# Second pass of a graph attention layer: the diagonal blocks transposed by VectorE from squares of 32, and the first block's rows normalized early

## The chip, the cores and the metric

The kernel runs on one core of a Trainium2 chip. The core has a matrix engine (TensorE, PE in the profile, with its weight loads as PEld), a vector engine (VectorE, DVE), an activation engine (ScalarE, ACT), a general engine (GpSimd, POOL), and SyncE (SP), which only issues DMAs here. Each engine works through its own list of instructions in order and waits for others by semaphores. On-chip memory is SBUF, and PSUM for the results of TensorE; DRAM is the large memory outside. Everything is fp32.

The metric is the device time of one run in microseconds, lower is better. Before the change it was 2959.15 us, the median of three runs from 2958.06 to 2962.82.

## The reference, cut to what matters

Two layers run on a matrix x of 4096 rows and 512 columns, with a 4096 x 4096 adjacency matrix. Only layer 0 and the beginning of layer 1 bear on the change:

```
h  = relu(layernorm(x))                      # layer 0
hw = h @ edge_w
e  = hw @ hw.T                               # 4096 x 4096, symmetric
e  = where(adj > 0, e, -9e15)
w  = softmax(h @ node_w, axis=0) * softmax(e, axis=1)
x  = x + (adj * w) @ (h @ weight) + bias
h  = relu(layernorm(x))                      # layer 1 begins
data1 = h @ W.T + b                          # then attention with 8 heads
```

## The kernel before, in words

Rows come in 32 tiles of 128 (P) and 8 blocks of 512 (BL), four tiles to a block (TB).

The first pass (until about 700 us) computes the scores e. As e is symmetric, only the blocks on and above the diagonal are computed and stored in DRAM, as e_d; in a diagonal block, tile row t is stored from its own diagonal tile to the right. The pass also takes the maximum of every row.

The second pass (about 700 to 1600 us) goes over 8 blocks b of 512 output rows, and inside each over the 32 tiles m of the other index: 256 steps. A step needs the scores of tile m against block b with tile m on the partitions. Where m's block lies above (m // TB < b), these are stored as they are needed, and a plain load (L396, tile et) brings them. Where it lies below (m // TB > b), the stored part is the transpose. Then `squares` (L402 to L411) brings four tiles at once with 16 DMAs of 64 KB each into a tile eb, so that every 32 x 32 square already stands at the place where it belongs, and VectorE's transpose, which works inside squares of 32, turns every square (L421, into the PSUM tile pt). In the diagonal block itself, `load` brings the stored upper part of four tiles by L392, also into an eb. The i-th tile of the block needs its first i*128 columns transposed; TensorE does this, one transpose of 128 x 128 for each (L427), 6 in a block.

After that, a step is the same for all: `masks` turns the adjacency tile a (loaded by L399) into 0 or -9e15 (L435); `exps` subtracts the row maximum (L441, in two parts where the tile was half turned), adds the mask (L442) and takes the exponential on ScalarE (L444); `weigh` multiplies by the adjacency (L450, tile at, 3 buffers), and GpSimd adds the exponentials up (L457, L460, tile racc); `gather` does four products of 128 x 128 by 128 x 512 into four PSUM tiles (L480, eight records a step).

The order is written out by hand. At step s each stage is called for a later step, "ahead" of s:

```
stages = ((load, 8), (squares, 9), (turn, 3), (exps, 2), (masks, 3), (weigh, 1), (gather, 0))
```

All engines get their instructions in this order. So at step s VectorE's list has the transpose of s+3, then L441 and L442 of s+2, the mask of s+3, L450 of s+1. All DMAs of loads and squares are on SP's list.

At the end of a block ScalarE copies the four results out of PSUM (L485), and in the next block `finish` scales one tile at a time and adds the residual (L499) and stores it to x1 (L500, on GpSimd's list): at steps 2 to 5 in blocks 1 and 2, at every second step from 2 on in later blocks. For blocks 1 to 6, named by SQ (L511), `finish` also takes the statistics for the layer norm of layer 1 (L505, L506). From step 10 of the following block `layernorm` then computes the square root (L517), scale and shift (L520, L522), the normalized rows (L526) and stores them with four DMAs a tile on SP's list (L532) in DRAM as h_d, again in an order that suits squares of 32.

The tail (about 1600 to 1720 us) is the first linear map of layer 1, one tile t a step: `fetch` (L552) reads h_d where t is in SQ, and x1 elsewhere. Where t is in SQ, `turn_h` is one transpose on VectorE (L577, same operation as L421). Elsewhere, tiles 0 to 3 and 28 to 31, the tail itself does statistics (L558, L560, L562), scale and shift (L568, L570), ReLU (L572), four transposes on TensorE (L583) and a copy from PSUM (L585). `linear` does the product (L591), `values` adds the bias (L598), which releases the PSUM tile; products on GpSimd (L602) and sums on VectorE (L607) follow.

Of the kernel before, what the change touches and what calls it, by code (L numbers as in the profile page):

```python
# [15 lines left out]
P = 128  # L16
# [12 lines left out]
def kernel(  # L29
# [15 lines left out]
    nc = tc.nc  # L45
# [6 lines left out]
    BL = 512  # L52
    NB = N // BL
    TB = BL // P
# [3 lines left out]
    ident = const.tile([P, P], FP, name="ident")  # L58
# [17 lines left out]
    S = 32  # L76
    e_d = dram.tile([N, N + 2 * S], FP, name="e_d")[:, 0:N]
# [23 lines left out]
    with tc.tile_pool(name="w0", bufs=1) as wp, tc.tile_pool(name="a0", bufs=2) as ap_, tc.tile_pool(  # L101
# [32 lines left out]
        def stats(t):  # L134
            st = sp.tile([P, 6], FP, name="st")
            nc.vector.bn_stats(st, xts[t])
            mvs[t] = sp.tile([P, 2], FP, name="mv")
            nc.vector.bn_aggr(mvs[t], st)
            sds[t] = sp.tile([P, 1], FP, name="sd")
            nc.scalar.activation(sds[t], mvs[t][:, 1:2], AF.Sqrt, bias=eps)  # L140

        def norm(t):
            rs = sp.tile([P, 1], FP, name="rs")
            nc.vector.reciprocal(rs, sds.pop(t))
            mr = sp.tile([P, 1], FP, name="mr")
            nc.vector.scalar_tensor_tensor(mr, mvs.pop(t)[:, 0:1], -1.0, rs, op0=ALU.mult, op1=ALU.mult)
            hs[t] = sp.tile([P, F], FP, name="h", bufs=5)
            if t < T0:
                nc.scalar.activation(hs[t], xts[t], AF.Relu, bias=mr, scale=rs)
            else:  # L150
                nc.scalar.activation(squares_of(hs[t]), columns_of(xts[t]), AF.Relu, bias=mr, scale=rs)
# [24 lines left out]
        def turn(t):  # L176
            b, j = divmod(t, TB)
            if j == 0:
                hts[b] = ap_.tile([P, KC, BL], FP, name="h_t")
            if t >= T0:  # L180
                nc.vector.transpose(
                    hts[b][:, :, j * P:(j + 1) * P].rearrange("p k (a q) -> p k a q", q=S),
                    hqs.pop(t).rearrange("p (a k q) -> p k a q", k=KC, q=S))
                return
            h = hs.pop(t)
            pt = pp.tile([P, KC, P], FP, name="pt")
            for k in range(KC):
                nc.tensor.transpose(pt[:, k, :], h[:, k * P:(k + 1) * P], ident)
            nc.vector.tensor_copy(hts[b][:, :, j * P:(j + 1) * P], pt)
            logit(t, h)  # L190
# [25 lines left out]
        def step(t):  # L216
            if t < NT:
                upto(fetch, t + 10 if t >= T0 else t + 7)
                upto(norm, t + 4)
                upto(send, t + 4)  # L220
                turn(t)
                upto(pull, t + 2)
                upto(stats, t + 5)
# [47 lines left out]
    def maxima(i, acc, psum, pool):  # L271

        mx = pool.tile([P, TB], FP, name="mx")
        nc.vector.tensor_reduce(mx, rm[:, i * TB:(i + 1) * TB, i:NB], AX.X, ALU.max)
        pc = psum.tile([P, TB, P], FP, name="pt")
        for j in range(TB):
            nc.tensor.transpose(pc[:, j, :], acc[:, j * P:(j + 1) * P], ident)
        cm = pool.tile([P, TB], FP, name="cm")
        nc.vector.tensor_reduce(cm, pc, AX.X, ALU.max)
        nc.vector.tensor_tensor(mx, mx, cm, ALU.max)  # L280
        yield
        pm = psum.tile([P, BL], FP, name="pt")
        nc.tensor.transpose(pm[:TB, 0:P], mx, ident)
        ms = pool.tile([TB, P], FP, name="ms")
        nc.vector.tensor_copy(ms, pm[:TB, 0:P])
        nc.gpsimd.dma_start(mx_d[i], ms)


    with tc.tile_pool(name="mx", bufs=1) as mxp, tc.tile_pool(name="b_a", bufs=6) as adjp, tc.tile_pool(
# [6 lines left out]
        loaded, masks = {}, {}  # L296
# [52 lines left out]
        for n in range(-6, len(items)):  # L349
# [3 lines left out]
            if n >= 0:  # L353
                i, j, t = items[n]
# [9 lines left out]
    with tc.tile_pool(name="c_a", bufs=11) as adjp, tc.tile_pool(name="c_b", bufs=4) as ebp, tc.tile_pool(  # L364
# [10 lines left out]
        src, pts, aj, mks, ex, at = {}, {}, {}, {}, {}, {}  # L375

        def rows_of(m):
            return slice(m * P, (m + 1) * P)
# [23 lines left out]
        def squares(b, m):  # L402
            cols = slice(b * BL, (b + 1) * BL)
            if m // TB > b and m % TB == 0:
                eb = ebp.tile([P, TB, BL], FP, name="eb")
                sq = e_d[cols, m * P:m * P + BL].rearrange("(a p) (i c q) -> i c p a q", p=S, q=S, i=TB)
                for i in range(TB):
                    for c in range(P // S):
                        nc.sync.dma_start(eb[c * S:(c + 1) * S, i, :].rearrange("p (a q) -> p a q", q=S), sq[i, c])
                for i in range(TB):  # L410
                    src[b, m + i] = eb  # L411

        def turn(b, m):

            i = m % TB
            eb = src[b, m]
            pt = p_t.tile([P, BL], FP, name="pt")
            pts[b, m] = pt
            parts = []
            if m // TB > b:  # L420
                nc.vector.transpose(pt, eb[:, i, :])  # L421
                src[b, m] = [(slice(0, BL), pt)]
                return
            n = i if m // TB == b else 0
            if n > 0:
                for j in range(n):
                    nc.tensor.transpose(pt[:, j * P:(j + 1) * P], eb[:, j, i * P:(i + 1) * P], ident)  # L427
                parts.append((slice(0, n * P), pt))
            if n < TB:
                parts.append((slice(n * P, BL), eb[:, i, :] if m // TB == b else eb))  # L430
            src[b, m] = parts
# [58 lines left out]
        def finish():  # L490

            t, acc, oc, rs, xt = left.pop(0)
            b, j = divmod(t, TB)
            if j == 0:
                sc = sp.tile([P, TB], FP, name="sc")
                nc.vector.reciprocal(sc, rs)
                nc.vector.tensor_tensor(sc, sc, na[:, b * TB:(b + 1) * TB], ALU.mult)
                scale[b] = sc
            nc.vector.scalar_tensor_tensor(oc, acc, scale[b][:, j:j + 1], xt, op0=ALU.mult, op1=ALU.add)  # L499
            nc.gpsimd.dma_start(x1[rows_of(t), :], oc)  # L500
            if t in SQ:
                if j == 0:
                    mv4[b] = sp.tile([P, TB, 2], FP, name="mv4", bufs=1), []
                st = sp.tile([P, 6], FP, name="st", bufs=4)
                nc.vector.bn_stats(st, oc)  # L505
                nc.vector.bn_aggr(mv4[b][0][:, j, :], st)  # L506
                mv4[b][1].append(oc)

        SQ = range(TB, (NB - 1) * TB)  # L511
        mv4 = {}

        def layernorm(b):
# [35 lines left out]
        def fetch(t):  # L550
            xl[t] = etp.tile([P, BL], FP, name="et")
            nc.sync.dma_start(xl[t], h_d[t] if t in SQ else x1[rows_of(t), :])  # L552

        def stats(t):
            if t in SQ:
                return
# [7 lines left out]
        def norm(t):  # L564
            if t in SQ:
                return
# [7 lines left out]
        def turn_h(t):  # L574
            if t in SQ:
                hts[t] = wkp.tile([P, BL], FP, name="d")
                nc.vector.transpose(hts[t].rearrange("p (k a q) -> p k a q", k=KC, q=S),  # L577
                                    xl.pop(t).rearrange("p (a k q) -> p k a q", k=KC, q=S))
                return
            h = hs.pop(t)  # L580
            pt = p_t.tile([P, BL], FP, name="pt")
            for k in range(KC):
                nc.tensor.transpose(pt[:, k * P:(k + 1) * P], h[:, k * P:(k + 1) * P], ident)  # L583
            hts[t] = wkp.tile([P, BL], FP, name="d")
            nc.scalar.copy(hts[t], pt)  # L585
# [27 lines left out]
        end = len(steps)  # L613
# [35 lines left out]

        stages = ((load, 8), (squares, 9), (turn, 3), (exps, 2), (masks, 3), (weigh, 1), (gather, 0))
        for s in range(-9, end):
            for f, ahead in stages:
                if 0 <= s + ahead < end:
                    f(*steps[s + ahead])
                if f is weigh:
                    b, m = divmod(s, NT)
                    if left and m > 1 and (m % 2 == 0 or b < 3):
                        finish()  # L660
                    if m == 10 and b - 1 in mv4:
                        norms = layernorm(b - 1)
                    if m >= 10:
                        next(norms, None)
                    tail(s - end)
                    if s == 3:
                        ending = maxima(NB - 1, acc_z, p_t, sp)
                    if s in (3, 4):
                        next(ending, None)
# [10 lines left out]
        pt = p_t.tile([P, BL], FP, name="pt")  # L680
# [50 lines left out]
    with tc.tile_pool(name="p", bufs=2) as prp, tc.tile_pool(name="rl", bufs=2) as rlp, tc.tile_pool(  # L731
# [321 lines left out]
        stages = ((load, 3), (logs, 5), (exps, 1), (weigh, 1), (factors, 2), (scale, 2), (gather, 0))  # L1053
# [47 lines left out]
```

## Time and profile before

One execution was profiled. Its page and its trace are the source of all times here.

| | |
|---|---|
| median of three runs | 2959.15 us |
| the profiled execution | 2957.07 us |
| its span | 2955.3 us |
| PE busy | 2911.4 us, 99% |
| DVE busy | 2534.6 us, 86% |
| POOL busy | 1380.0 us, 47% |
| ACT busy | 1325.5 us, 45% |
| L480 PE, x2048 | 887.2 us |
| L427 PE, x48 | 9.1 us, 274 ns each |
| L421 DVE, x112 | 80.6 us, 719 ns each |
| L577 DVE, x24 | 16.8 us, 699 ns each |
| L409 SP, squares, x448 | 64 KB each |
| granted TensorE clock | 0.995 |

Busy time is the sum over an engine's instructions. A matmul's recorded length is longer than its share of TensorE's time, because matmuls overlap: L480's 2048 records have a mean of 594 ns, yet fill 887.2 us. What a stage costs is therefore read from the distance between starts, and from the idle times, which the timeline shows in brackets with what ended them. A clock below 1 means that TensorE was granted only that share of its full rate.

### The profile page before, as it was taken

How to read it: one execution, taken by the hardware profiler on the slowest of the kernel's cores; microseconds unless marked ns; L12 is line 12 of the kernel's file. 1: busy time of each engine (PE TensorE's matmuls, PEld its weight loads, DVE VectorE, ACT ScalarE, POOL GpSimd, SP SyncE). 2: the span in 40 equal slices, each digit the busy share in tenths (PEclk: the TensorE clock that was granted, in tenths of full speed). 3: DMA queues.
4: the chain of work that ended last, by engine and by line, in shares of the span. 5: the costliest groups of instructions: out<-in, count | busy, mean ns of one | idle time of the engine just before them, and what ended most of it. 6: DMA issues, size and time to landing. Idle time of an engine off the chain costs nothing.

```text
span 2955.3 us, 42955 instructions
## 1 busy us (share of the span) xinstructions
PE 2911.4 (99%) x15179; PEld 1137.7 (38%) x15179; DVE 2534.6 (86%) x3584; ACT 1325.5 (45%) x1822; POOL 1380.0 (47%) x1043
## 2 busy tenths in 40 slices
PE   8999999999999999999999989999999999999998
PEld 4444444444444444444444423323222322232222
DVE  5435777778888998998996789999999999999998
ACT  2211111111121221221221068888777777777776
POOL 3401111113444444444444756565757575757574
PEclk9999999999999999999999999999999999999999
DMA  5525666667876766756653259696969696979795
GB/s 181 172 78 200 223 218 225 226 218 187 205 178 162 177 161 187 186 166 180 190 167 127 61 152 242 187 258 188 256 191 249 194 250 204 243 202 243 208 232 153
DMA packets 485160, 570.89 MB, mean 193 GB/s; under 512 B 265080, under 2 KB 315288, under 8 KB 484944
## 3 DMA queue, kind: packets, MB, share of 16 engines
q1 hardware_dynamic: 431920, 406.70, 45.8%
q0 software_dynamic: 51008, 157.51, 23.2%
q10 hardware_dynamic: 2016, 3.93, 0.4%
q8 instruction: 119, 1.95, 0.3%
q14 instruction: 97, 0.79, 0.1%
HBM read 415.76 MB, written 72.55 MB: 165 GB/s over the span
## 4 chain that ended last, share of the span: by engine, by line
PE 92%; DVE 4%; ACT 2%; DMA 1%; issue 1%; SPq 0%; POOL 0%; DVEq 0%; ACTq 0%; POOLq 0%
PE po L480 29%; PE pv L881 27%; PE pe L331 15%; PE dn L886 9%; PE po L591 4%; PE ps L196 3%; PE pe L203 3%; DVE pr L849 2%; PE pt L936 1%; ACT e L817 1%; DMA acc<-pr 1%; DMA xt<-in_x_dram 0%; DVE acc_z L154 0%; DVE pt L441 0%; PE pt L920 0%
## 5 line engine op out<-in xcount | busy, mean ns | idle before, releaser
L881 PE MATMUL pv<-pr,sup 128*32 128x512 f32 x8192 | 1010.0, 594 | 9.0 <-POOL d_m L1046 5.4
L480 PE MATMUL po<-sup,at 128*128 128x512 f32 x2048 | 887.2, 594 | 3.8 <-DVE at L450 3.8
L858 POOL TENSOR_TENSOR acc<-acc,pr 128x1024 f32<-128x1024 f32 x232 | 558.2, 2406 | 318.1 <-DVE pr L849 317.8
L849 DVE SCALAR_TENSOR_TENSOR pr<-z,g_m,ex 128x1024 f32<-128x1024 f32 x512 | 631.0, 1273 | 5.2 <-ACT ex L807 4.1
L480 PEld LDWEIGHTS po<-sup,at 128*128 128x128 f32 x2048 | 387.1, 190 | 483.2 <-issue 446.3
L460 POOL TENSOR_TENSOR racc<-racc,ex 128x512 f32<-128x512 f32 x240 | 362.3, 1510 | 385.3 <-ACT ex L444 383.8
L881 PEld LDWEIGHTS pv<-pr,sup 128*32 128x32 f32 x8192 | 286.7, 110 | 593.2 <-issue 533.6
L444 ACT ACTIVATE ex<-d 128x512 f32<-128x512 f32 x256 | 160.5, 630 | 624.7 <-DVE d L442 616.5
L331 PE MATMUL pe<-he_t,he_t 128*128 128x512 f32 x896 | 386.4, 592 | 0.0
L807 ACT ACTIVATE ex<-e 128x1024 f32<-128x1024 f32 x256 | 263.0, 1027 | 227.2 <-DVE pr L849 226.6
L849 DVE SCALAR_TENSOR_TENSOR pr<-z,g_m,e 128x1024 f32<-128x1024 f32 x256 | 328.9, 1285 | 9.9 <-PE pv L881 5.9
L886 PE MATMUL dn<-pr,d_m 128*2 128x512 f32 x1984 | 335.6, 592 | 0.0
L817 ACT ACTIVATE e<-e,ld_m 128x1024 f32<-128x1024 f32 x256 | 291.0, 1137 | 6.5 <-DMA e<-in_adj_t_dram 6.3
L846 DVE SCALAR_TENSOR_TENSOR pr<-rl,ngd_m,ex 128x1024 f32<-128x1024 f32 x224 | 285.0, 1273 | 1.6 <-ACT ex L807 1.2
L835 ACT ACTIVATE rl<-z,ngd_m,d_m 128x1024 f32<-128x1024 f32 x224 | 275.0, 1228 | 0.0
L450 DVE TENSOR_TENSOR at<-ex,a 128x512 f32<-128x512 f32 x256 | 189.5, 740 | 71.1 <-ACT ex L444 48.0
L331 PEld LDWEIGHTS pe<-he_t,he_t 128*128 128x128 f32 x896 | 169.2, 190 | 210.1 <-issue 190.5
L335 POOL DMA_DIRECT2D e_d<-es x144 | 78.4, 545 | 364.8 <-ACT es L334 359.2
L334 ACT COPY es<-pe 128x512 f32<-128x512 f32 (+2 forms) x144 | 79.1, 550 | 377.2 <-PE pe L331 377.2
L442 DVE TENSOR_TENSOR d<-pt,mk 128x512 f32<-128x512 f32 x256 | 177.0, 691 | 8.8
L336 DVE CUSTOM_DVE_ANT_0 mk<-pe,mk 128x512 f32<-128x512 f32 (+2 forms) x144 | 93.0, 645 | 98.9 <-ACT es L334 98.8
L435 DVE TENSOR_SCALAR mk<-a 128x512 f32<-128x512 f32 x256 | 128.5, 502 | 2.2 <-DMA a<-in_adj_t_dram 2.2
(186 smaller groups left out, 2564.9 us busy)
## 6 DMA issues: line engine op xcount, KB each, us to landing
e<-in_adj_t_dram SPq DMA_DIRECT2D x256, 512.0 KB, 5.5
acc<-pr POOLq DMA_DIRECT2D x152, 512.0 KB, 5.7
a<-in_adj_t_dram SPq DMA_DIRECT2D x256, 256.0 KB, 3.8
ar<-in_adj_dram SPq DMA_DIRECT2D x120, 256.0 KB, 3.0
e_d<-es POOLq DMA_DIRECT2D x120, 256.0 KB, 3.1
eb<-e_d SPq DMA_DIRECT2D x456, 64.0 KB, 3.0
ac<-in_adj_t_dram SPq DMA_DIRECT2D x112, 256.0 KB, 3.5
et<-e_d SPq DMA_DIRECT2D x112, 256.0 KB, 3.8
```

The source lines that it names most:

```text
L331: nc.tensor.matmul(pe[:, :w], he_t[i][:, k, (t % TB) * P:(t % TB + 1) * P], he_t[j][:, k, BL - w:], start=(k == 0), stop=(k == KC - 1))
L450: nc.vector.tensor_tensor(w, e, aj.pop((b, m)), ALU.mult)
L460: nc.gpsimd.tensor_tensor(racc, racc, e, ALU.add)
L480: nc.tensor.matmul(po[j], w[:, j * P:(j + 1) * P], sup[:, m, :], start=(m == 0), stop=last)
L807: nc.scalar.activation(x_, ra.pop((i, m)), AF.Exp)
L817: nc.scalar.activation(x_, ra[i, m], AF.Exp, bias=ld_m[:, h // HG, m:m + 1])
L835: nc.scalar.activation(r, zs_[i, 0], AF.Relu, bias=ngd_m[:, h // HG, m:m + 1], scale=d_m[:, h, m:m + 1])
L846: nc.vector.scalar_tensor_tensor(w, rl.pop((i, m)), ngd_m[:, h // HG, m:m + 1], x_, op0=ALU.subtract, op1=ALU.mult)
L849: nc.vector.scalar_tensor_tensor(w, zs_[i, k], g_m[:, h + k, m:m + 1], e3.pop((i, m)) if k == 3 else x_, op0=ALU.max, op1=ALU.mult)
L858: nc.gpsimd.tensor_tensor(acc[i, 3], acc[i, 3], w, ALU.add)
L881: nc.tensor.matmul(v[c][q][r * D + c0:r * D + c0 + Q, :], va[:, m, g * HG + k, c0:c0 + Q], pr[i, m, k][:, q * BL:(q + 1) * BL], start=(m = ...
L886: nc.tensor.matmul(dn[r * Q:r * Q + w.shape[1], :], w, src[:, q * BL:(q + 1) * BL], **fl)
```

## The change

Three things change, all in the second pass and the tail.

First, the diagonal blocks get what the blocks below it had. For tile i of a diagonal block (i = 1, 2, 3), `squares` now issues four DMAs of i*16 KB on SP, which bring the stored part above the diagonal as squares of 32 into the unused left part of the same eb. `turn` calls VectorE's transpose on the first i*128 columns, in place of i transposes on TensorE.

Second, `squares` is called 8 steps ahead in place of 9, so that it follows `load` of the same step, which makes the tile eb that it fills; the loop starts at -8.

Third, SQ now begins with tile 0. The rows of block 0 get their statistics in `finish` and are normalized and stored to h_d in block 1; the tail reads h_d for tiles 0 to 3 and turns them on VectorE. Tiles 28 to 31 stay as they were.

```diff
@@ squares
+            if m // TB == b and m % TB > 0:
+                i = m % TB
+                sq = e_d[b * BL:b * BL + i * P, m * P:(m + 1) * P].rearrange("(a p) (c q) -> c p a q", p=S, q=S)
+                for c in range(P // S):
+                    nc.sync.dma_start(
+                        src[b, m][c * S:(c + 1) * S, i, 0:i * P].rearrange("p (a q) -> p a q", q=S), sq[c])
@@ turn
-            if m // TB > b:
-                nc.vector.transpose(pt, eb[:, i, :])
-                src[b, m] = [(slice(0, BL), pt)]
-                return
-            n = i if m // TB == b else 0
+            n = TB if m // TB > b else i if m // TB == b else 0
             if n > 0:
-                for j in range(n):
-                    nc.tensor.transpose(pt[:, j * P:(j + 1) * P], eb[:, j, i * P:(i + 1) * P], ident)
+                nc.vector.transpose(pt[:, 0:n * P], eb[:, i, 0:n * P])
                 parts.append((slice(0, n * P), pt))
@@
-        SQ = range(TB, (NB - 1) * TB)
+        SQ = range((NB - 1) * TB)
@@
-        stages = ((load, 8), (squares, 9), (turn, 3), (exps, 2), (masks, 3), (weigh, 1), (gather, 0))
-        for s in range(-9, end):
+        stages = ((load, 8), (squares, 8), (turn, 3), (exps, 2), (masks, 3), (weigh, 1), (gather, 0))
+        for s in range(-8, end):
```

## The prediction

> **What bounds the kernel now.** I read four views, in this order: the chain of work that ended last, the TensorE timeline of the stretch that the change touches (from 697 us to 1722 us), the VectorE timeline around the places where TensorE stops, and SP's timeline at the start of the second pass. The chain of the whole page:
>
> ```profile
> PE 92%; DVE 4%; ACT 2%; DMA 1%; issue 1%; SPq 0%; POOL 0%; DVEq 0%; ACTq 0%; POOLq 0%
> ```
>
> The TensorE timeline says where TensorE is not the bound. Columns are start, length, engine, line, operation, then the idle time before it and what ended that:
>
> ```profile
> 705.75 12.85 PE L480 MATMUL po<-sup,at 128*128 128x512 f32 x24 [2.25 <-DVE at L450]
> ...
> 826.42 3.60 PE L480 MATMUL po<-sup,at 128*128 128x512 f32 x8
> 829.86 0.38 PE L427 MATMUL pt<-ident,eb 128*128 128x128 f32 x2
> 830.07 3.60 PE L480 MATMUL po<-sup,at 128*128 128x512 f32 x8
> 833.51 0.49 PE L427 MATMUL pt<-ident,eb 128*128 128x128 f32 x3
> 833.84 92.87 PE L480 MATMUL po<-sup,at 128*128 128x512 f32 x216
> ...
> 952.14 3.70 PE L480 MATMUL po<-sup,at 128*128 128x512 f32 x8 [0.40 <-DVE at L450]
> ...
> 957.17 3.70 PE L480 MATMUL po<-sup,at 128*128 128x512 f32 x8 [1.10 <-DVE at L450]
> ...
> 1604.45 5.40 PE L591 MATMUL po<-eb,d 128*128 128x512 f32 x8 [1.85 <-ACT d L585]
> ```
>
> TensorE runs without a gap except at four places: before the first product of the pass, twice in block 2, where VectorE's L450 is late, and at the hand-over to the tail. A step of eight products takes 3.43 us (92.7 us for 27 steps in the chain). From 826.42 to 830.07 is 3.65 and from 830.07 to 833.84 is 3.77, so one L427 transpose costs TensorE 0.11 us and not its recorded 0.27.
>
> The third view is VectorE's timeline in blocks 1 and 2:
>
> ```profile
> 826.96 1.86 DVE L441 TENSOR_TENSOR pt<-eb,mb 128x384 f32<-128x384 f32 x1
> ...
> 834.78 0.71 DVE L421 STREAM_TRANSPOSE pt<-eb 128x512 f32<-128x512 f32 x1
> 835.40 0.53 DVE L441 TENSOR_TENSOR pt<-pt,mb 128x384 f32<-128x384 f32 x1
> ...
> 937.70 0.69 DVE L505 BATCH_NORM_STATS2 st<-oc 128x6 f32<-128x512 f32 x1
> 938.43 0.18 DVE L506 BATCH_NORM_AGGREGATE mv<-st 128x2 f32<-128x6 f32 x1
> ```
>
> A 384-wide L441 with both inputs in SBUF takes 1.86 us where 0.57 is its undisturbed time (703.47). POOL's L460 runs from 827.11 to 828.39 in its timeline, and L441 ends 0.4 us after it. Whatever VectorE does just before such a collision is free until POOL is done.
>
> **What the Trainium skill says.** "SBUF — State Buffer", section "SBUF: two separate sides": VectorE and GpSimd share a port pair as an exclusive lock, and a VectorE operation with two SBUF inputs blocks for the whole of a GpSimd operation that reads SBUF. The 1.86 us agrees. "TensorE: Matmul & The Clock Gate", Part 1: a free-running activity window of 3.413 us decides the clock, which halves after an idle window. The trace agrees: the clock is 0.50 from 705.75 to 710.40 and 0.69 from 1605 to 1610. Part 4 of that page: transposes do not count as busy for this. The hand-over fits, for it went to half clock although eight transposes ran inside its gap. "VectorE: DVE Perf Modes", "The three transpose paths": VectorE transposes only within 32x32 blocks, so the block order has to come from elsewhere. Here that is the squares DMA.
>
> **The change part by part.** Everything below is against the profiled run: 2957.07 us, its span 2955.3.
>
> *TensorE's diagonal transposes go.* There are 6 per block (1+2+3), 0.11 us each: 0.66 us a block, 5.3 us in all where TensorE is the bound. In block 0 all six ran before 705.75, while TensorE was waiting, so nothing comes back there.
>
> *VectorE's transposes come.* The 128x512 row is 720 ns, 0.63 us start to start. No narrower one is in the trace. By a straight quarter the first would be 0.18 us; if the fixed part of L441's widths (295, 428, 544, 668 ns) holds, 0.32. I take 0.23, 0.37 and 0.50 start to start, 1.1 us a block.
>
> *Twelve more DMAs a block on SP* (four each of 16, 32 and 48 KB). Issues there take 0.43 us (L532) to 0.53 us (spacing of the 64 KB squares when nothing holds them): 5 to 6.4 us a block.
>
> *Statistics of block 0 in block 1.* L505 and L506 lengthen a finish from 0.66 to 1.6 us, four times, 3.8 us. On ScalarE there are two table loads of 1.28 us and four L526 of 0.8, on VectorE two small operations of 0.4 us, on SP 16 stores of 0.43 us. In block 2 the same work (ScalarE 969 to 993) brings no gap on TensorE after 961. I cost it at nothing beyond the 3.8 us.
>
> *Squares at 8 ahead.* Each 16-DMA group goes one step (3.43 us) later. In block 1 the group of m=24 would now follow a store that waits for L526, and starts near 871 us. Its first four land near 877 (2.1 issue, 3.0 landing), and VectorE needs them near 889: 12 us of cover.
>
> Now by place.
>
> Block 0. VectorE reaches L450 for the first product at 705.01, now behind two more transposes: 0.6 us later. The half clock ends when a busy window ends, on average half a window plus one later, 5.1 us instead of 4.65: 0.2 us more. SP issues in this stretch without rest:
>
> ```profile
> 695.00 13.07 SPq L409 DMA_DIRECT2D eb<-e_d  x16
> 708.12 1.91 SPq L399 DMA_DIRECT2D a<-in_adj_t_dram  x4
> ```
>
> With twelve issues and a4 ahead, the group of m=4 ends near 714, so mask tile a5 is issued there and lands near 717.5 (3.4 to 3.8 us). VectorE wants it at 715.4, then delivers product 3 at 718.6; TensorE needs it at about 718.9. This just fits. I put block 0 at +0.9, from +0.5 to +4.
>
> Block 1. Here L450 has little lead: for product 7 it ends at 842.5, the product starts at 844.13. I walked VectorE through the steps with the added work. The second transpose and the first statistics end at 827.5, inside POOL's lock until 828.39: free. The third adds nothing before 833.3 for the same reason. From then on each finish costs its 0.95 more: L450 for product 6 ends at 840.0 (needed 840.04, TensorE now being 0.66 earlier), for product 7 at 844.6 (needed 843.47). That is a stall of 1.2 us; later steps have VectorE at 2.87 against 3.43. Net +0.5. If nothing were hidden it would be +3; with no stall, -0.7.
>
> Block 2. L450 for product 7 stays at 956.43, as the transposes fall into L441's waits (1.84, 1.37, 1.12). Only the last 0.33 us is gained: -0.3.
>
> Blocks 3 to 7. In block 3 L450 is 0.4 to 2 us ahead at the diagonal, and each extra transpose is covered by that or by a lock. 5 x 0.66 = -3.3.
>
> Hand-over. The last product ends at 1601.76, the last L499 at 1602.5. Now come reciprocal, statistics, L572 on ScalarE, eight transposes, L585 and at 1604.45 L591. After: L577 on VectorE right behind L499 (699 ns), L591 at about 1603.25: -1.2. The transposes of the next two tiles, 8 x 0.11: -0.9. The gap without products was 2.7 us and becomes 1.5. Block 2's waits of 0.40 and 1.10 us, 1.6 us with the transposes, did not lower the clock, so I take it that this one does not either. The first eight L591 then take 3.6 instead of 5.4: -1.8. Together -3.9; -2.1 if the clock drops all the same. VectorE's L577 for the third tile follows L598 and ends two microseconds ahead of its product.
>
> Sum: 0.9 + 0.5 - 0.3 - 3.3 - 3.9 = -6.1 us, so 2951.0 for a run like the profiled one. The median shown is 2.1 us above that run; the same -6.1 gives 2953.0.
>
> **The rivals.**
> The clock falls at the hand-over after all. For it: a window that holds the whole gap is busy for 56% only (1.9 of 3.413 us). Counting windows from 710.40, where full clock returned, the one from 956.2 to 959.6 held 2.4 us of products (71%) and the clock stayed; the one from 1601.3 to 1604.7 held 0.7 (20%) and it fell. It gives 2954.8.
> SP is late in block 0. For it: single issues of 2.09 us there while the DMA engines are over 90% busy. Against it: a4 now goes out before the big group instead of behind it. Every microsecond that a5 is later than 717.8 is a microsecond of stall; at 2 to 5 us it gives 2955 to 2958.
> More is hidden. Block 1's stall does not arise (+0.5 becomes -0.7) and block 0 starts no later: 2950.9.
> Slower: the squares become late. SP's load with stores, in blocks 1 and 2, is 16 x 0.53 + 4 x 0.47 + 8 x 0.43 = 13.8 us per four steps of 13.7 us, so lost lead is not won back while the stores last. If groups issue at block 0's 0.82 us, they take 18.4, and over two groups nearly the 12 us of cover are gone. From there every microsecond stops VectorE's L421, then TensorE. It ends slower when about 12 us of stall come together in the blocks with both; 2966. Against it: the trace shows 0.82 only in the first group, and 8.4 to 9.6 us for a group in block 1.
>
> **How the numbers follow.** Chances: as worked out 0.45, clock falls 0.20, SP late 0.17, more hidden 0.10, squares late 0.08. Under 0.2% (5.9 us) is about what a measurement of this kernel can't tell from no change. The likeliest case lies on that line: a little over half of it is faster (0.25), with 0.02 of the second and all 0.10 of the fourth: 0.37. Slower: 0.08 and 0.01 of SP's tail. Same: 0.54. The likeliest case alone spans 2951 to 2955; the range takes in the fourth below and SP's late start above, 2950 to 2960.5.
>
> **What would show it.** No L427; 48 L421 at widths of 128, 256 and 384, 0.2 to 0.6 us. TensorE's line unbroken around the diagonal of blocks 3 to 7, those blocks 0.66 us shorter. A stall by L450 of about 1 us in block 1 near product 7. L591 starting 1.5 us after the last L480, at full clock. Wrong would be: waits of L421 or L435 on DMAs past 720 us, a first L480 more than 1 us later, or stalls in blocks 3 to 7.

## The result, and the profile after

The changed kernel takes 2953.49 us, the median of 18 runs (2950.86 to 2954.88); on the same chip the kernel before takes 2957.82 us, the median of 18 runs (2954.96 to 2962.82). The ratio is 0.9984, with an interval from 0.9978 to 0.9991: some 4.3 us faster, between 2.7 and 6.5. The predicted time was 2953.0. The gain of 0.16% is below the 0.2% that the prediction called hard to tell from no change; with 18 runs of each, the interval excludes 1. The profiled execution took 2953.74 us, with a span of 2951.9 us.

The first view is again the chain of work that ended last:

```profile
PE 80%; DVE 8%; issue 5%; DMA 3%; ACT 2%; POOL 1%; SPq 0%; DVEq 0%; POOLq 0%; ACTq 0%
```

TensorE's share fell from 92% to 80%. That is not the change: 4 points each were lost in L331 of the first pass (15% to 11%) and in L881 of the later attention (27% to 23%, now L882), where the code is the same and the chain went through other engines this time. TensorE is busy for 98% of the span, against 99%. The chain can't show a change of this size, so I read TensorE's timeline of the second pass (columns: start, length, engine, line, operation, then the idle time before it and what ended it). From L435 on all line numbers are one higher than before; L416 are the new DMAs, and L428 is VectorE's transpose (L421 before). "Product 7" stands for the products of step 7 of a block, eight records, so x256 are 32 steps.

```profile
705.45 13.21 PE L481 MATMUL po<-sup,at 128*128 128x512 f32 x24 [6.12 <-DMA eb<-e_d]
...
815.18 0.95 PE L478 MATMUL rs<-ones,racc 128*128 128x1 f32 x8
815.99 27.85 PE L481 MATMUL po<-sup,at 128*128 128x512 f32 x64
845.05 82.67 PE L481 MATMUL po<-sup,at 128*128 128x512 f32 x192 [1.22 <-DVE at L451]
...
953.16 3.70 PE L481 MATMUL po<-sup,at 128*128 128x512 f32 x8 [0.51 <-DVE at L451]
...
958.18 82.67 PE L481 MATMUL po<-sup,at 128*128 128x512 f32 x192 [1.32 <-DVE at L451]
...
1090.28 62.07 PE L481 MATMUL po<-sup,at 128*128 128x512 f32 x144 [0.47 <-DVE at L451]
...
1152.99 110.11 PE L481 MATMUL po<-sup,at 128*128 128x512 f32 x256
...
1601.24 38.03 PE L592 MATMUL po<-eb,d 128*128 128x512 f32 x88 [1.46 <-DVE d L578]
```

No transpose is left among the products. Block 4 is one unbroken run of 256 records (1152.99); before, the diagonal's transposes cut every such run. Two waits are new: one in block 1, before product 7, and one in block 3, before product 13. The bracket of the first product of the pass names a DMA, but the product starts 0.06 us after L451 on VectorE ends (704.71 to 705.39).

The two traces are compared piece by piece, by landmarks on TensorE that both kernels have: the last L283 of the first pass, the row sums at the end of each block (before L477, after L478), and the first transpose L645 (after L646) behind the first linear map's beginning.

| piece, us | before | after | measured | predicted |
|---|---|---|---|---|
| block 0 | 115.23 | 116.12 | +0.89 | +0.9 |
| block 1 | 111.42 | 112.38 | +0.96 | +0.5 |
| block 2 | 113.46 | 113.13 | -0.33 | -0.3 |
| block 3 | 111.42 | 111.50 | +0.08 | -0.66 |
| blocks 4 to 7 | 445.80 | 443.10 | -2.70 | -2.64 |
| hand-over | 47.66 | 43.82 | -3.84 | -3.9 |
| sum | 945.00 | 940.05 | -4.95 | -6.1 |

What lies outside these pieces holds the same code, and moves by itself: the first pass ended 0.84 us earlier, and from that L646 to TensorE's last instruction it took 2.4 us longer (1303.40 against 1300.97; the other runs below lie between 1301.08 and 1303.8). A single pair of spans therefore says nothing at the level of one microsecond. The pieces do.

What makes the new wait in block 1 stands in VectorE's timeline:

```profile
821.46 0.32 DVE L428 STREAM_TRANSPOSE pt<-eb 128x128 f32<-128x128 f32 x1
821.69 1.53 DVE L442 TENSOR_TENSOR pt<-eb,mb 128x512 f32<-128x512 f32 x1
...
827.25 0.46 DVE L428 STREAM_TRANSPOSE pt<-eb 128x256 f32<-128x256 f32 x1
827.62 0.27 DVE L442 TENSOR_TENSOR pt<-pt,mb 128x128 f32<-128x128 f32 x1
827.92 0.97 DVE L442 TENSOR_TENSOR pt<-eb,mb 128x384 f32<-128x384 f32 x1
...
839.40 0.68 DVE L451 TENSOR_TENSOR at<-ex,a 128x512 f32<-128x512 f32 x1
...
841.51 0.18 DVE L507 BATCH_NORM_AGGREGATE mv<-st 128x2 f32<-128x6 f32 x1
842.04 0.73 DVE L428 STREAM_TRANSPOSE pt<-eb 128x512 f32<-128x512 f32 x1 [0.35 <-DMA eb<-e_d]
...
844.31 0.68 DVE L451 TENSOR_TENSOR at<-ex,a 128x512 f32<-128x512 f32 x1
```

GpSimd's timeline has, at the second transpose:

```profile
827.17 1.28 POOL L461 TENSOR_TENSOR racc<-racc,ex 128x512 f32<-128x512 f32 x1
```

The transposes of 128 and 256 columns take 0.32 and 0.46 us, and the next instruction starts 0.23 and 0.37 us after they do. Those start-to-start costs are the ones that the prediction took. The second one is free, as predicted: L442 behind it now takes 0.97 us where it took 1.86, and ends 0.44 us after GpSimd's L461 (827.17 to 828.45), as before (0.43). So the port lock of "SBUF — State Buffer", "SBUF: two separate sides", pays for it. L451 for product 7 ends at 844.99, and the product starts at 845.05. One wait was not foreseen: VectorE stood still for 0.35 us before 842.04. The bracket puts it down to a DMA of squares, but the four DMAs that this transpose reads were issued by 813.8 and had landed by 815.8. They belong to the first of these groups on SP's list:

```profile
808.50 9.51 SPq L409 DMA_DIRECT2D eb<-e_d  x16
818.11 1.86 SPq L399 DMA_DIRECT2D a<-in_adj_t_dram  x4
820.02 9.56 SPq L409 DMA_DIRECT2D eb<-e_d  x16
```

What landed at 842 was a later group. The cause of this stop is open.

The bracket of 1.22 us counts from the recorded end of the product before, which overhangs. From product 31 of block 0 (815.99) to product 7 are 29.07 us, and 27.55 in a kernel below whose block 1 has no wait. So product 7 is 1.52 us late, and product 8 loses 0.10 more, as after the waits in blocks 2 and 3: 1.62 us in all.

### The profile page after: what moved, and what is told of

The parts are those of the page before. It is cut to its first block, busy times and chain, and to the rows that moved or that the text cites. A ratio compares the mean times of both kernels' runs of the same rounds, so it can differ in the third digit from the quotient of the medians.

```text
span 2951.9 us, 43009 instructions
## 1 busy us (share of the span) xinstructions
PE 2904.7 (98%) x15115; PEld 1135.7 (38%) x15115; DVE 2541.1 (86%) x3606; ACT 1324.7 (45%) x1817; POOL 1376.2 (47%) x1043
## 4 chain that ended last, share of the span: by engine, by line
PE 80%; DVE 8%; issue 5%; DMA 3%; ACT 2%; POOL 1%; SPq 0%; DVEq 0%; POOLq 0%; ACTq 0%
PE po L481 27%; PE pv L882 23%; PE pe L331 11%; PE dn L887 8%; DVE pr L850 4%; PE po L592 4%; PE ps L196 3%; PE pe L203 3%; DMA acc<-pr 2%; DVE pt L442 1%; POOL e_d L335 1%; PE pt L937 1%; DVE pr L847 1%; POOL acc L859 1%; ACT e L818 0%
## 5 line engine op out<-in xcount | busy, mean ns | idle before, releaser
L882 PE MATMUL pv<-pr,sup 128*32 128x512 f32 x8192 | 1008.9, 594 | 10.1 <-POOL d_m L1047 5.6
L481 PE MATMUL po<-sup,at 128*128 128x512 f32 x2048 | 885.4, 594 | 9.6 <-DMA eb<-e_d 6.1
L481 PEld LDWEIGHTS po<-sup,at 128*128 128x128 f32 x2048 | 388.5, 190 | 498.4 <-issue 452.8
L461 POOL TENSOR_TENSOR racc<-racc,ex 128x512 f32<-128x512 f32 x240 | 357.4, 1489 | 385.4 <-ACT ex L445 384.0
L882 PEld LDWEIGHTS pv<-pr,sup 128*32 128x32 f32 x8192 | 289.0, 110 | 592.8 <-issue 526.3
L331 PE MATMUL pe<-he_t,he_t 128*128 128x512 f32 x896 | 386.4, 592 | 0.0
L331 PEld LDWEIGHTS pe<-he_t,he_t 128*128 128x128 f32 x896 | 169.2, 190 | 210.1 <-issue 190.5
L451 DVE TENSOR_TENSOR at<-ex,a 128x512 f32<-128x512 f32 x256 | 187.5, 732 | 71.0 <-ACT ex L445 45.9
L442 DVE TENSOR_TENSOR pt<-et,mb 128x512 f32<-128x512 f32 x112 | 127.5, 1138 | 0.0
```

The source lines that it names most:

```text
L331: nc.tensor.matmul(pe[:, :w], he_t[i][:, k, (t % TB) * P:(t % TB + 1) * P], he_t[j][:, k, BL - w:], start=(k == 0), stop=(k == KC - 1))
L451: nc.vector.tensor_tensor(w, e, aj.pop((b, m)), ALU.mult)
L461: nc.gpsimd.tensor_tensor(racc, racc, e, ALU.add)
L481: nc.tensor.matmul(po[j], w[:, j * P:(j + 1) * P], sup[:, m, :], start=(m == 0), stop=last)
L882: nc.tensor.matmul(v[c][q][r * D + c0:r * D + c0 + Q, :], va[:, m, g * HG + k, c0:c0 + Q], pr[i, m, k][:, q * BL:(q + 1) * BL], start=(m = ...
```

## The experiments

Two theories stood at first. Theory A is the prediction's: the change in the diagonal gives 0.11 us per transpose wherever TensorE is the bound, and the stall of block 1 comes from the statistics of block 0's rows. Theory B holds VectorE's new transposes responsible for the stall.

### One part alone: the diagonal

In the changed kernel, block 0's rows are left to the tail again:

```diff
-        SQ = range((NB - 1) * TB)
+        SQ = range(TB, (NB - 1) * TB)
```

> The changed kernel without the rows of block 0 (SQ from tile 4 again). From block start to block start (L478 to L478) the changed kernel takes 112.38 us for block 1, the kernel before 111.42. Theory A, the stall of block 1 comes from the statistics of block 0, while the diagonal transposes hide behind GpSimd's lock: no wait for L451 in block 1, the block 110.8 us. Rival B, the stall comes from the transposes' VectorE time: a wait of 1 us or more stays, the block about 112. Both: block 0 0.9 us longer than before, blocks 4 to 7 at 110.75, the hand-over (last L478 to L646) 47.7 as before. In all about 2.5 us faster than before under A, 1.5 under B.

2953.92 us, the median of 21 runs, against 2958.03 (41 runs) of the kernel before; ratio 0.9987, from 0.9981 to 0.9994. TensorE's timeline has no listed wait in block 1:

```profile
816.15 110.37 PE L481 MATMUL po<-sup,at 128*128 128x512 f32 x256
...
1601.26 3.70 PE L592 MATMUL po<-eb,d 128*128 128x512 f32 x8 [1.85 <-ACT d L586]
```

Block 1 took 111.01 us: 0.41 less than before and 1.37 less than with both parts. It is not quite down to the 110.76 of an undisturbed block. The missing 0.25 us are again at product 7: its L451 ends at 843.79, the product starts 0.15 us late, too little to be listed, and product 8 loses the 0.10. So the listed stall needs the statistics, and Theory B falls as the whole cause. With the transposes alone 0.25 us of stall are left.

The second line is a surprise. With the old form of the hand-over and the same gap of 1.85 us as before, the first eight products took 3.70 us, not 5.40. The clock did not fall, and the hand-over took 45.96 us in place of 47.66. More on this below.

### One part alone: the rows

In the kernel before, SQ begins with tile 0; the diagonal stays on TensorE and the squares stay 9 steps ahead.

```diff
-        SQ = range(TB, (NB - 1) * TB)
+        SQ = range((NB - 1) * TB)
```

> The kernel before with the rows of block 0 alone (SQ from tile 0, TensorE's transposes kept, squares 9 ahead). Theory A: block 1 has a wait of 0.5 to 0.8 us for L450 at product 7, the block about 112.1 us in place of 111.42. Rival B: no wait, 111.4. Both: block 0 as before (115.2 from the last L283 to the first L477), blocks 4 to 7 as before at 111.45, the hand-over at 43.8 in place of 47.7, its first products at full clock. In all about 3 us faster than before.

2955.14 us (13 runs) against 2958.03; ratio 0.999, from 0.9982 to 0.9998. Block 1 keeps its transposes on TensorE, and waits less, because TensorE itself is later:

```profile
843.94 82.67 PE L480 MATMUL po<-sup,at 128*128 128x512 f32 x192 [0.32 <-DVE at L450]
```

Block 1 took 112.01, blocks 4 to 7 from 111.42 to 111.57 as before, and the hand-over 43.82, exactly that of the whole change. So the hand-over's gain belongs to the rows and the gain of blocks 4 to 7 to the diagonal. By the medians the two parts are faster by 4.1 and 2.9 us alone and by 4.3 together. That they are worth less together than their sum is mainly block 1: the stall at product 7 is 0.25 us with the transposes alone, 0.59 with the statistics alone and 1.62 with both.

### The remaining gap at the hand-over

In the changed kernel the first two tiles of the tail are turned ahead of the last `finish` calls, and not in the tail's first step:

```diff
+        turn_h(0)
+        turn_h(1)
         while left:
             finish()
...
-                if s == 0:
-                    turn_h(0)
-                if s + 1 < NT:
+                if 0 < s and s + 1 < NT:
```

> The changed kernel with the first two transposes of the tail (L578) moved on VectorE's list ahead of the four L500 of the last block; VectorE is idle for 6.9 us there. If the gap of 1.46 us ahead of the first L592 is the wait for VectorE's list, it goes, since the first L592 then waits only for the first L500: the hand-over 42.4 us in place of 43.8, the kernel 1.5 us faster than the changed one. Rival: L592 also waits for the later L500s through the PSUM tiles or for the load of w1, and the gap stays above 1 us.

2950.27 us (9 runs) against 2958.03; ratio 0.9974, from 0.9964 to 0.9984. VectorE's timeline, and then TensorE's:

```profile
1589.14 1.30 DVE L578 STREAM_TRANSPOSE d<-et 128x512 f32<-128x512 f32 x2
```

```profile
1595.93 3.68 PE L481 MATMUL po<-sup,at 128*128 128x512 f32 x8
1599.45 25.91 PE L592 MATMUL po<-eb,d 128*128 128x512 f32 x60
```

L592 follows the last L481 without a gap, and the hand-over takes 42.09 us, 1.73 less. In the changed kernel both transposes stand behind the four L500, although their rows had been in DRAM since block 1:

```profile
1597.24 3.33 DVE L500 SCALAR_TENSOR_TENSOR oc<-po,sc,xt 128x512 f32<-128x512 f32 x4 [0.59 <-PE po L481]
1600.48 1.29 DVE L578 STREAM_TRANSPOSE d<-et 128x512 f32<-128x512 f32 x2
```

The gap of 1.46 us is thus made by the order of VectorE's list alone.

### Finishes two steps apart

In blocks 1 and 2 `finish` ran at every step from 2 to 5; here it runs at every second step, as in the later blocks:

```diff
-                    if left and m > 1 and (m % 2 == 0 or b < 3):
+                    if left and m > 1 and m % 2 == 0:
```

> The changed kernel with finish at every second step from step 2 on in blocks 1 and 2 too, as in the later blocks. Theory A: VectorE is late in blocks 1 and 2 because four finishes with statistics come in four steps; spread out, the waits for L451 in both blocks go: block 1 110.8 us in place of 112.38, block 2 111.3 in place of 113.13, the kernel 3.4 us faster than the changed one. Rival: at steps 6 and 8 of block 1 the steps have full transposes and VectorE has only 0.56 us to spare in each, so the wait only moves: block 1 stays above 111.5.

2949.32 us (9 runs) against 2958.03; ratio 0.9976, from 0.9967 to 0.9986.

```profile
816.19 110.11 PE L481 MATMUL po<-sup,at 128*128 128x512 f32 x256
...
965.56 72.37 PE L481 MATMUL po<-sup,at 128*128 128x512 f32 x168 [0.59 <-DVE at L451]
```

Block 1 is one run of 256 records, 110.76 us, 1.62 less than in the changed kernel; block 2 takes 111.62, 1.51 less, with one wait left. The stalls of both blocks come from four finishes in a row, each with its statistics on VectorE. With 0.95 us more at every second step the work fits in the lead.

### A wider gap and the clock

The prediction had put 1.8 us of the hand-over down to the clock: a gap of 2.7 us lets it fall, one of 1.5 us does not. In the changed kernel VectorE turns the tail's first tile twice more, with the same result, before the second:

```diff
                 if s == 0:
                     turn_h(0)
+                    for _ in range(2):
+                        nc.vector.transpose(hts[0].rearrange("p (k a q) -> p k a q", k=KC, q=S),
+                                            x_0.rearrange("p (a k q) -> p k a q", k=KC, q=S))
```

> The changed kernel with the first transpose of the tail done three times over on VectorE (same result), which makes the gap ahead of the first L592 about 2.75 us in place of 1.46, near the 2.7 us without products of the kernel before. Theory A: the half clock after the gap belongs to the gap's length; the first eight L592 take 5.4 us and the hand-over 46.9 us (43.8 + 1.3 + 1.8). Rival B: it is decided by where the gap falls against free-running windows, so that with the same length it can come or not; without it the hand-over is 45.1 us. One run can show B and not exclude it.

One run, 2953.36 us, against 2957.01 (9 runs). TensorE's timeline, and then its window from 1605 to 1610 (stretch, length, then busy time and instructions of PE, PEld, DVE, ACT and POOL, the granted clock, the DMA share, GB/s), of this kernel:

```profile
1603.23 22.16 PE L592 MATMUL po<-eb,d 128*128 128x512 f32 x51 [2.96 <-DVE d L639]
```

```profile
1605.00:1610.00 5.00, 5.00 (x13) 2.28 (x12) 1.31 (x2) 0.00 (x0) 2.25 (x2) 1.00 0.33 106
```

The same window of the kernel before:

```profile
1605.00:1610.00 5.00, 5.00 (x11) 2.14 (x10) 0.12 (x1) 0.00 (x0) 0.00 (x0) 0.69 0.16 54
```

With 2.96 us without products the clock stayed at 1.00; in the trace of before, with 2.7 us from the recorded end of the last L480 to the first L591, it fell to half until 1608. The hand-over took 45.32 us, which is the 43.82 plus the 1.50 of the longer gap. So the length of the gap alone doesn't decide the fall, and 1.8 us are not saved in every run.

### Block 0 left on TensorE

In block 0 the diagonal is turned by TensorE, without the 12 DMAs of squares; all else is the change.

```diff
-            if m // TB == b and m % TB > 0:
+            if m // TB == b > 0 and m % TB > 0:
...
-                nc.vector.transpose(pt[:, 0:n * P], eb[:, i, 0:n * P])
+                if m // TB == b == 0:
+                    for j in range(n):
+                        nc.tensor.transpose(pt[:, j * P:(j + 1) * P], eb[:, j, i * P:(i + 1) * P], ident)
+                else:
+                    nc.vector.transpose(pt[:, 0:n * P], eb[:, i, 0:n * P])
```

> The changed kernel with the diagonal transposes of block 0 alone on TensorE again and without their 12 DMAs. Theory: two transposes ahead of the first L451 on VectorE's list cost block 0 0.53 us, and the rest of its 0.9 is the half clock. The first product then starts 5.86 us after the last L283 in place of 6.39, and the piece from L283 to the first L478 is 115.2 to 115.6 us in place of 116.1. Rival: SP's 12 more DMAs make it late; then the first product is no earlier, but waits on mask tiles after 712 us in the changed kernel would be gone.

One run, 2949.87 us, against 2957.01 (9 runs). Its lines from L435 on stand four further down than in the changed kernel.

```profile
705.02 12.13 PE L485 MATMUL po<-sup,at 128*128 128x512 f32 x24 [2.25 <-DVE at L455]
...
843.19 82.67 PE L485 MATMUL po<-sup,at 128*128 128x512 f32 x192 [0.87 <-DVE at L455]
```

The first product comes 5.86 us after L283, as in the kernel before, and not 6.39. Block 0 takes 114.51 us, less than was expected, since the half clock here lasted 3.41 us and 6.83 in all other profiles. The bracket in block 1 falls from 1.22 to 0.87 us, by the 0.35 us that VectorE stood still before 842.04; that stop is gone. It stands before the same transpose in both other kernels whose block 1 is that of the change (841.92 with the early turns, 842.47 with the wider gap). In this kernel VectorE's list is another one from block 0 on. It fits that the stop goes with the list; why it comes is not shown.

### Squares 8 steps ahead, alone

In the kernel before only the distance is changed:

```diff
-        stages = ((load, 8), (squares, 9), (turn, 3), (exps, 2), (masks, 3), (weigh, 1), (gather, 0))
-        for s in range(-9, end):
+        stages = ((load, 8), (squares, 8), (turn, 3), (exps, 2), (masks, 3), (weigh, 1), (gather, 0))
+        for s in range(-8, end):
```

> The kernel before with the squares 8 steps ahead in place of 9 and nothing else. By the prediction it costs nothing, since the first transfers of a group land 12 us before they are needed: all blocks within 0.1 us of the kernel before (115.2 or 115.5 for block 0, then 111.4, 113.5, 111.4, 111.4), no wait of L421 on a DMA. Rival: VectorE's L421 waits on squares in blocks 1 or 2, which are then more than 0.3 us longer.

One run, 2959.5 us, against 2957.01 (9 runs from 2955.79 to 2961.46). Blocks 1 to 7 take what they took before, within 0.03 us, and VectorE waits for no DMA between 700 and 930 us. What makes the total higher lies outside the pass: its first pass ended at 701.57 and the rest took 1303.8 us. So the shorter distance costs nothing by itself. This is also the third hand-over in the old form, and the clock stayed again:

```profile
1605.78 3.70 PE L591 MATMUL po<-eb,d 128*128 128x512 f32 x8 [1.86 <-ACT d L585]
```

It took 45.97 us, as in the kernel with the diagonal alone.

### All waits at once

Finishes two steps apart, the tail's first turns ahead of the last finishes, block 0 on TensorE, and the layer norm of the rows from step 20 of a block instead of 10 (lines again four further down):

```diff
-                    if m == 10 and b - 1 in mv4:
+                    if m == 20 and b - 1 in mv4:
...
-                    if m >= 10:
+                    if m >= 20:
```

> The changed kernel with the four repairs together: finish at every second step, the layer norm's scale and rows from step 20 of a block on in place of 10, the tail's first two transposes ahead of the last four L500, block 0's diagonal on TensorE. If the waits seen in the changed kernel are all there is between it and an unbroken TensorE, block 1 is 110.8, block 2 110.8 to 111.1, block 3 110.8, the hand-over 42.1, block 0 115.2 to 115.6: 6.9 us less than the changed kernel, a ratio to the kernel before of about 0.996. Rival: moved statistics and rows meet the later steps with full transposes and waits for L451 show up there.

2947.69 us (5 runs, 2945.54 to 2948.41) against 2957.01 (9 runs); ratio 0.9965, from 0.9951 to 0.9978. It is the fastest kernel measured here.

```profile
814.27 110.11 PE L485 MATMUL po<-sup,at 128*128 128x512 f32 x256
...
963.69 72.37 PE L485 MATMUL po<-sup,at 128*128 128x512 f32 x168 [0.64 <-DVE at L455]
...
1036.70 110.11 PE L485 MATMUL po<-sup,at 128*128 128x512 f32 x256
...
1594.02 37.93 PE L596 MATMUL po<-eb,d 128*128 128x512 f32 x88
```

The pass takes 933.7 us, 6.35 less than with the change and 11.3 less than before (1.7 of these are the clock of the hand-over, which fell in one profile of three). One wait is left, in block 2, where finishes at steps 6 and 8 meet the diagonal at steps 8 to 11. The line at 1036.70 settles block 3. There the changed kernel's VectorE, and then GpSimd, stand so:

```profile
1085.72 0.17 DVE L521 RECIPROCAL rs<-sd 128x4 f32<-128x4 f32 x1
1085.92 0.16 DVE L523 SCALAR_TENSOR_TENSOR mr<-mv,rs 128x4 f32<-128x4 f32 x1
1086.10 0.59 DVE L428 STREAM_TRANSPOSE pt<-eb 128x384 f32<-128x384 f32 x1
1087.04 1.52 DVE L442 TENSOR_TENSOR pt<-eb,mb 128x256 f32<-128x256 f32 x1
...
1089.54 0.69 DVE L451 TENSOR_TENSOR at<-ex,a 128x512 f32<-128x512 f32 x1
```

```profile
1087.01 1.26 POOL L461 TENSOR_TENSOR racc<-racc,ex 128x512 f32<-128x512 f32 x1 [3.29 <-ACT ex L445]
```

Scale and shift of the layer norm (0.4 us) fall into the same steps as the diagonal. With the new transposes ahead of it, L442 reaches its SBUF half at 1087.04, just after GpSimd has begun at 1087.01, and takes 1.52 us where 0.43 is its free time. Before, the same half (L441) ran at 1084.91 in 0.43 us, and GpSimd began only at 1085.46. L451 for product 13 ends at 1090.23; the bracket is 0.47 us, and the product starts 0.63 us late. Without the layer norm there, block 3 has no wait and takes 110.76 us; with it, in the kernel that only has its finishes two steps apart, a wait of 0.45 remained.

## Why the prediction was right, and where not

**The diagonal's transposes on TensorE, 0.11 us each.** Right. Blocks 4 to 7 are shorter by 0.67 us each, six times 0.11, and only in kernels with the new diagonal.

**VectorE's transposes at 0.23, 0.37 and 0.50 us.** Right: 0.23 (821.46 to 821.69), 0.37 (827.25 to 827.62), and 0.50 for the 384-wide one at 832.15. The straight quarter that the prediction had as the other bound (0.18) is ruled out. That the lock hides them in block 1 is right as well, but for the 0.25 us that they cost there without statistics.

**Block 0, +0.9.** Right: +0.89. The first product is 0.53 us later where 0.6 was said, and the kernel with block 0 on TensorE takes that back. The rest is the half clock, which ran for 5.35 us of products (705.45 to 710.80) in place of 4.63 (705.75 to 710.38); half of the difference is 0.36. That it came out at the predicted size is luck, as it depends on where the half clock happens to end. Over all profiles block 0 takes 114.51 to 115.44 us with TensorE's transposes there and 115.55 to 116.12 with VectorE's, 0.8 us apart in the mean (5 each). SP did not make TensorE wait: its group of squares took 9.44 us and the mask a5 went out at 710.96, ahead of the 714 that the prediction had.

```profile
701.47 9.44 SPq L409 DMA_DIRECT2D eb<-e_d  x16
710.96 1.91 SPq L399 DMA_DIRECT2D a<-in_adj_t_dram  x4
```

The rival in which SP stalls TensorE falls with that. It took the 0.82 us per issue of the kernel before for this group; it was 0.59. But one of the signs of error that the prediction had named did come: past 720 us VectorE waited twice for a mask, 1.81 us at 754.65 and 0.32 at 766.90. TensorE shows no gap there.

```profile
754.65 0.60 DVE L436 TENSOR_SCALAR mk<-a 128x512 f32<-128x512 f32 x1 [1.81 <-DMA a<-in_adj_t_dram]
```

**Block 1, +0.5.** The mechanism was right, the size not. In the kernel with block 0 on TensorE, which lacks VectorE's stop of 0.35 us, product 7 is 1.16 us late where 1.2 was said. In the changed kernel L451 for product 6 ends at 840.08 where 840.0 was said, and for product 7 at 844.99 where 844.6 was said: the walk missed the 0.35 us before 842.04 and hardly anything else. With the 0.10 lost at product 8 the stall is 1.62 us, which less the 0.66 saved gives the +0.96. The rival in which more is hidden falls too.

**Block 2, -0.3, and blocks 4 to 7.** Right.

**Block 3, -0.66.** Wrong: +0.08. The step that failed is "each extra transpose is covered by that or by a lock". I had compared the transposes with the leads of L450 one by one, and left out that the layer norm's two operations fall into the same steps, and that a later L441 can run into a GpSimd operation that it used to miss. A lock hides what stands ahead of it only while the order of the two stays the same.

**The hand-over, -3.9.** The total is right with -3.84 for this pair of profiles, and two of its three terms are right for any: L591 earlier by 1.27 (1.2 said), and 0.87 for the transposes of the next tiles (0.9 said), together the 2.14 between 45.96 and 43.82. The third term, -1.8 for the clock, is 1.70 in this pair, but only because the profiled execution of before had the half clock there. Two other executions of the old hand-over, with the same gap, had not, and a gap as long in the new form kept full clock too. The step that failed is the rule taken from the share of products in one window. The window of 20% fell, but counted in the same steps of 3.413 us, each time from the return of full clock, one of 20% did not fall in the diagonal's kernel (1597.85 to 1601.27), nor one of 28% in the kernel with squares 8 ahead. Counted so in all ten traces, the 20 windows with at most 17% of products all fell, 12 of the 18 between 20% and 40% fell, and none above 40% did. The window of the changed hand-over has 57%, those of the wider gap 60% and 53%. So the shorter gap saves the chance of a fall, not 1.8 us in every run. What decides between 20% and 40% stays open. The rival in which the clock falls after the change came about in none of the four profiles with the gap of 1.46 us.

Without the clock the pieces give -3.3 us, and the medians give -4.3 with an interval from -6.5 to -2.7, which holds it. That the time came out within 0.5 us is luck. The change was put at 6.1 us and is 4.3 by the medians, but the three runs from which the prediction started had a median 1.3 us above that of all 18. The clock's term and the losses left out in blocks 1 and 3 do not offset each other: both made the forecast gain too large.

**Squares late.** It did not come about. Past 720 us one bracket of VectorE names squares, the one at 842.04, and these had landed long before.

## What to carry to other kernels

Before work is moved to an engine with some lead, walk that engine's list in every stage where it meets other periodic work: here the gain of 0.67 us a block was whole in the four blocks where nothing else fell on the diagonal, and lost in the two where statistics or a layer norm did. Reordering the lists around it, with block 0 left on TensorE, then gave 6.35 us in the pass, more than the 4.95 of the change. And don't book a clock effect that one profile shows as a gain: look for it in a second execution of the same code. When a bracket names a DMA, check when the data that the instruction reads had landed.

## What was not expected of the hardware

The granted clock after a short gap varies from run to run. With 2.7 us without products at the hand-over it fell to half for 3.4 us in one profile of three, at a cost of 1.7 us (47.66 against 45.96 and 45.97), and with 2.96 us in another form it did not fall. "TensorE: Matmul & The Clock Gate", Part 1, has a free-running window decide, and Part 4 has transposes not count. That the window's phase against the gap varies would fit the scatter, and where few or many products fell into a window the counts above agree. They do not settle the cases between: two windows with 20% of products went different ways.

The other is a collision: VectorE's two-input operation starting 0.03 us behind GpSimd's took 1.52 us in place of 0.43. Here a start just after the other's cost VectorE 1.1 us.
